# New duration and hand-over constants in the list schedule of a four-layer image kernel

## The chip, the cores and the metric

One Trainium2 chip, of which the kernel uses one core. The metric is the device time of one execution in microseconds (us); less is better. The time before is 11614.76 us, the median of three executions (11599.19 to 11631.03). One more execution was profiled: 11598.44 us, of which 11596.7 us lie between its first and its last instruction (the span).

## The reference, cut to what matters

The input `x` has 32 images of 512 channels and 32 by 32 pixels, in float32. Four layers follow each other, and each adds its result to its input: `x = x + layer(group_norm(x))`.

```python
# layer 0: 2-D DCT of every channel, normalised, averaged; a two-layer perceptron gives one factor a channel
weights = sigmoid(relu(x_avg @ w1.T) @ w2.T);  return x * weights[:, :, None, None]
# layer 1: grouped 3x3 convolution, 32 groups
# layer 2: 1x1 conv -> x, z;  f1 = 1x1 conv(x), f2 = 2x2/2 conv(f1), f3 = 2x2/2 conv(f2)
def step(h, inp):                     # state-space scan along the pixels, 256 channels x 16 states
    da, dbx, c = inp
    h = h * da + dbx
    return (h, einsum('bdn,bn->bd', h, c))
# run forward and backward on f1, f2, f3; layer norm; the coarse results are added to the finer ones;
# times silu(z), and a last 1x1 conv
# layer 3: channel attention from a deformable 3-tap sampling over the channel means
```

The scan of layer 2 is the heart of the work: for each image 256 channels by 16 states by 1024 pixels in two directions on `f1`, and the same on the smaller `f2` and `f3`.

## The kernel before

**A plan, then the program.** The kernel does not write its instructions down in the order in which the text stands. It first records operations with `pe`, `act`, `dve`, `pool` and `dma`, one helper for each engine (matrix, scalar, vector and GpSimd engine, and the queue SP that issues DMAs). Each record has a duration that the author states, a key (when it is due, in hundredths of an image), and the buffers that it reads and writes. Then `Plan.order` plays a list schedule: it keeps a clock, lets each engine take the ready operation with the lowest key, marks it as busy for the stated duration, and releases the operations that depend on it after a hand-over time. The order in which operations are taken becomes the program order of every engine's queue, and the same pass gives each buffer its slot. On the chip each queue runs strictly in that order and waits on semaphores. So the stated durations and hand-over times cost nothing themselves; they decide only who stands before whom, and which slot a buffer has.

**The constants.** `SAME` is the hand-over to the same engine, `CROSS` to another engine within the scan loops (`fine` and `both`), `BESIDE` to another engine everywhere else, `QUEUE` to an operation that issues a DMA. `t_mm`, `t_dve`, `t_act` and `t_pool` turn a number of elements into a duration; many matrix operations have a number of their own.

The lines where the plan uses them:

```python
for u in o.users:
    u.waits -= 1
    if not u.waits:
        lat = self.SAME if u.eng == o.eng and o.eng != "SP" else u.cross
        heapq.heappush(events, (now + lat, u.seq, 0, u))
...
if e == "SP":
    idle[e] = now + o.dur
    dma = max(dma, now + 2.0) + o.size / 240e3
    o.end = dma + 1.2
else:
    idle[e] = o.end = now + o.dur
```

**One scan unit.** An image has 84 units of 128 partitions by 1024 elements: 32 for the forward scan on `f1` (`fine`, first half), 20 for the coarse scans of the next image (`lower`, through `both`), 32 for the backward scan on `f1` (`fine`, second half). A unit on `f1` is this chain: the matrix engine spreads B into the PSUM buffer `pb` (L1220, two matmuls), ACT makes the decay `da` by an exponential (L1227), DVE multiplies `pb` by `dt` (L1233) and scans (L1166, `h` from `da` and `pb`), POOL multiplies `h` by C (`cb`, L1241), and after each four units the matrix engine adds four `h` into the accumulators `y0` and `y1b` (L1249). In the coarse scans the same steps have the lines L1347 and L1354, L1389 and L1398, L1361, L1409 and L1419. There are two `pb`, two `da`, two `cb`, six `h`, four `dt`, and one of each accumulator; a unit can begin only when the unit that held its slot is through.

**Work beside.** All other work is laid between the units by its key: the transforms of layer 0 three images ahead (`spectra`, L455 to L639; images after the fourth are taken in groups of four), the grouped convolution of layer 1 (`front`, L853), the dense layers (`dense`, L906; `down_conv`, L928), the inputs of the scans (`prepare`, L1013 to L1075), the layer norms (L1096 to L1119), the output (L1494 to L1511) and layer 3 (`back`, L1552 to L1658; its twelve weighted sums an image are L1618 on ACT and L1624 on DVE). The keys, such as `FRONT` or `LN_LATE`, and the choice of engine for each operation are not touched.

Of the kernel before, what the change touches and what calls it, by code (L numbers as in the profile page):

```python
# [59 lines left out]
class Plan:  # L60
# [3 lines left out]

    SAME, CROSS, BESIDE, QUEUE = 0.06, 0.2, 0.5, 2.0

    def __init__(self, rings):
        self.rings = rings  # L70
# [45 lines left out]
    def order(self):  # L116
# [35 lines left out]
        while events:  # L152
            now = events[0][0]
            touched = set()
            while events and events[0][0] <= now:
                _, _, kind, o = heapq.heappop(events)
                if kind == 0:
                    heapq.heappush(ready[o.eng], (o.key, o.seq, o))
                    touched.add(o.eng)
                elif kind == 1:  # L160
                    touched.add(o)
                else:
                    done += 1
                    for b in o.bufs:
                        b.left -= 1
                        if b.ring and not b.left:
                            free[b.ring].append(b.slot)
                            wake(b.ring, touched)
# [5 lines that stand above are left out]
            again = True  # L174
            while again:
                again = False
                for e in engines:
                    while idle[e] <= now and ready[e]:
                        _, _, o = heapq.heappop(ready[e])
                        n = lacks(o)  # L180
                        if n is not None:
                            parked[n].append(o)
                            continue
                        woken = set()
                        o.acq = [b for b in o.acq if b.slot is None]
                        for b in sorted(o.acq, key=lambda b: b.key):
                            b.slot = free[b.ring].pop(0)
                            if b.ring in line:
                                line[b.ring].pop()
                                wake(b.ring, woken)  # L190
                        again = again or bool(woken)
                        o.start = now
                        issued.append(o)
                        if e == "SP":
                            idle[e] = now + o.dur
                            dma = max(dma, now + 2.0) + o.size / 240e3
                            o.end = dma + 1.2
                        else:
                            idle[e] = o.end = now + o.dur
                        heapq.heappush(events, (idle[e], o.seq, 1, e))  # L200
                        heapq.heappush(events, (o.end, o.seq, 2, o))
        stuck = [o for o in self.ops if o.start is None]
# [14 lines left out]


def t_mm(n, count=1):
    return count * (1.0 * n / 512 + 0.03)  # L220


def t_dve(n):
    return 0.075 + n / 960


def t_act(n, ptr=False):
    return 0.09 + n / 1180 + (0.06 if ptr else 0.0) + (0.12 if n > 1000 else 0.0)


def t_pool(n):
# [4 lines left out]
def kernel(ctx: ExitStack, tc: tile.TileContext, t: dict, out: bass.AP):  # L236
# [228 lines left out]
    def root(dst, v, n, bufs, key):  # L465

        pool(
            lambda: nc.gpsimd.tensor_tensor(dst(), v(), mhalf[:, 0:n], ALU.pow), 175, bufs, bufs, key
        )

    def group_stats(mean, var, gm, rstd, q, w, key, read, write, n=CT):


        ps = mm()
        pe(
            lambda: nc.tensor.matmul(ps.t[:, 0:n], lhsT=gavg, rhs=mean(), start=True, stop=True),
            0.25, read, [ps], key,
        )
        dve(lambda: nc.vector.tensor_sub(q(), mean(), ps.t[:, 0:n]), n, [*read, ps], write, key)
        act(lambda: nc.scalar.copy(gm(), ps.t[:, 0:n]), n, [ps], write, key)  # L480
        act(lambda: nc.scalar.activation(q(), q(), AF.Square), n, write, write, key)
        p2 = mm()

        def sums():
            nc.tensor.matmul(p2.t[:, 0:n], lhsT=gavg, rhs=q(), start=True, stop=False)
            nc.tensor.matmul(p2.t[:, 0:n], lhsT=gavg, rhs=var(), start=False, stop=True)

        pe(sums, 0.5, [*read, *write], [p2], key)
        dve(lambda: nc.vector.tensor_scalar_add(w(), p2.t[:, 0:n], 1e-5), n, [p2], write, key)
        root(rstd, w, n, write, key)  # L490

# [15 lines left out]
    def spectra(b, k0, k1):  # L507
        for c in range(CT):
# [37 lines left out]
            for step in range(2):  # L546


                for h in range(2 * step):
                    ps = mm()  # L550

                    def turn(ps=ps, h=h, sx=sx):
                        for j in range(4):
                            i = (h * 4 + j) * P
                            nc.tensor.transpose(
                                ps.t[:, j * P : (j + 1) * P], sx.t[:, 0, i : i + P], ident
                            )

                    pe(turn, 0.7, [a], [ps], key)
                    act(  # L560
                        lambda ps=ps, h=h, sx=sx: nc.scalar.copy(sx.t[:, 1, halves[h]], ps.t), HB,  # L561
                        [ps], [z[h]], key,
                    )
                for h in range(2):
# [7 lines left out]
                                start=True, stop=True,  # L572
                            )

                    pe(dcts, 1.05, [z[h], *([st] if step == 0 else [])], [ps], key)
                    if step == 0:
                        def put(ps=ps, h=h, sx=sx, b=b, c=c):
                            dst = sx.t[:, 0, :].rearrange("p (k r) -> p r k", k=IMG)
# [71 lines left out]
    def channel_weights(b0, n, key):  # L650
# [8 lines left out]
        for h in range(2):  # L659
            w, wf = weights(b0)  # L660
            dma(
                lambda wf=wf, h=h: nc.sync.dma_start(
                    wf().rearrange("p (c m) -> p c m", c=CT), t["w1"][:, :, h * HB : (h + 1) * HB]
                ),
                P * 8192, [], [w], key,
            )
            ps = mm()
            for m in range(4):
                def up(wf=wf, ps=ps, m=m):
                    for c in range(CT):  # L670
                        nc.tensor.matmul(
                            ps.t[:, m * n : (m + 1) * n],
                            lhsT=wf()[:, c * HB + m * P : c * HB + (m + 1) * P],
                            rhs=sg.t[:, 0:n, 2, c], start=(c == 0), stop=(c == CT - 1),
                        )

                pe(up, 0.9, [w, *st], [ps], key)
            act(
                lambda ps=ps, h=h: nc.scalar.activation(
                    sm.t[:, h * 4 * n : (h + 1) * 4 * n], ps.t[:, 0 : 4 * n], AF.Relu  # L680
                ),
                4 * n, [ps], [(sm, "hid")], key,
            )
        for h in range(2):
# [8 lines left out]
            for m in range(2):  # L693
                for k0 in (0, 4):
# [5 lines left out]
                                start=(k == 0), stop=(k == 7),  # L700
                            )

                    pe(down, 0.9, [w, (sm, "hid")], [ps], key)
            e = slice(8 * n, 10 * n)
            sigmoid_to(
                lambda h=h: sg.t[:, 0:n, 5, 2 * h : 2 * h + 2],
# [20 lines left out]
    def front(b, S, k0, k1):  # L727
# [38 lines left out]
                        start=True, stop=True,  # L766
                    )

        pe(blocks, 1.2, [sm], [ps], k0, [sk])
        act(lambda ps=ps: nc.scalar.copy(sk.t[:, 0:48], ps.t[0:96, 0:48]), 48, [ps], [(sk, 0)], k0)  # L770

        def by_block(i):
# [21 lines left out]
        for c in range(CT):  # L794
# [44 lines left out]
            for h in range(2):  # L839
# [9 lines left out]
                for n, dy in enumerate((1, 0, 2)):  # L849
# [11 lines left out]
                                start=(n == 0), stop=(n == 2),  # L861
                            )

                    pe(conv, 1.2, [wk, pk], [ps], key, [xb])


                act(
# [33 lines left out]
    def dense(w, rhs, m, cols, reads, ps, key, acq=(), opened=False):  # L901


        for k, r in enumerate(rhs):
# [3 lines left out]
                    start=(k == 0 and not opened), stop=(k == len(rhs) - 1),  # L908
                )

            pe(f, t_mm(HB), [*reads[0], reads[1][k]], [ps], key, acq)

    def down_conv(lv, f, side, S, key):

# [4 lines left out]
        for m in range(2):  # L919
            ps = mm()  # L920
            for k in range(2):
                for q0 in (0, 2):
# [8 lines left out]
                                start=(k == 0 and q == 0), stop=(k == 1 and q == 3),  # L931
                            )

                    pe(part, 2 * max(t_mm(n), 0.25), [w, f], [ps], key, [fo])
            act(
                lambda m=m, ps=ps: nc.scalar.activation(
                    fo.t[:, m, :], ps.t[:, 0:n], AF.Identity, bias=c_b[lv - 1][:, m : m + 1]
# [248 lines left out]
    def fine(lv, f, pre, S, rev, ck):  # L1186
# [8 lines left out]
        for d in range(2):  # L1195
# [10 lines left out]
            for k in range(NS // NQ):  # L1206
# [7 lines left out]
                for q in range(4):  # L1214
# [3 lines left out]
                    def bcast(pb=pb, k=k):  # L1218
# [15 lines left out]
                        [dt[q], pb], [pb], ck.key(DB_AHEAD),  # L1234
                    )
                    pl.op(
                        "DVE", 2.2, lambda h=h, da=da, pb=pb: scan(h.t, da.t, pb.t, rev), [da, pb], [h],
                        ck.key(),
                    )
                    pool(  # L1240
# [5 lines left out]
                for i, cols in enumerate(halves):  # L1246
# [4 lines left out]
                                start=(k == 0), stop=(k == NS // NQ - 1),  # L1251
                            )

                    pe(add, 1.15, hs, [acc[i]], ck.key(2))
            y = pl.buf("yv")
            yv.append(y)
            dma(
# [45 lines left out]
    def both(lv, f, pre, ysum, below, n, ck):  # L1303
# [24 lines left out]
        for d in range(2):  # L1328
# [11 lines left out]
            for k0 in range(0, 4, nk):  # L1340
# [15 lines left out]
                                start=True, stop=True,  # L1356
                            )

                pe(bcast, 0.6 if nk == 1 else 0.8, [sb], [pb], ck.key(B_AHEAD))
                dve(  # L1360
                    lambda pb=pb, quads=quads: nc.vector.tensor_mul(  # L1361
                        pieces(pb.t),
# [16 lines left out]
                for r in range(2):  # L1379
# [14 lines left out]
                    else:  # L1394
# [7 lines left out]
                                n, [(dt, 1)], [(da, q)], ck.key(6), True,  # L1402
                            )
                    pl.op(
                        "DVE", 2.2, lambda h=h, da=da, pb=pb, r=r: scan(h.t, da.t, pb.t, r == 1),
                        [da, pb], [h], ck.key(),
                    )
                    pool(
# [13 lines left out]
                                    start=(k0 + k == 0), stop=False,  # L1422
                                )

                    pe(add, 0.65 if nk == 1 else 1.4, [h], [acc[r]], ck.key(2))
                    ck.u += 1
            dg = skip_weights(lv, d, ck.key(8))
            for r in range(2):
# [1 line left out]
                    lambda r=r, d=d, dg=dg: nc.tensor.matmul(  # L1430
                        accv(r)[:, d, 0:n], lhsT=dg.t, rhs=f.t[:, d, :], start=False, stop=True
                    ),
                    max(t_mm(n), 0.22), [f, dg], [acc[r]], ck.key(2),
                )
        y = pl.buf("yv" if n > 64 else "yc")

# [87 lines left out]
    def back(b, S, k0, k1):  # L1524
        sm, xo = S["smb"], S["xo"]

        def at(i):
            return k0 + (k1 - k0) * i
# [29 lines left out]
                ps.t[:, 2 * CT : 3 * CT], lhsT=ident, rhs=yv(), start=True, stop=True  # L1558
            )

        pe(shift, 1.1, n_, [ps], at(0.2))
        for i in range(3):
            def op_(i=i):
                return npos()[:, 4 * i : 4 * i + 4]
# [31 lines left out]
                    rhs=ident, start=True, stop=True,  # L1596
                )

        pe(rows, 1.2, n_, [ps2], at(0.2), [gt])
        act(lambda: nc.scalar.copy(gt.t[:, 0, :], ps2.t), HB, [ps2], [(gt, 0)], at(0.2))  # L1600

        for c in range(CT):
            for i in range(3):
# [3 lines left out]
                def hat():  # L1607
# [17 lines left out]
                        pr.t, in0=pr.t, in1=gt.t[:, 0, :], op0=ALU.mult, op1=ALU.add, scale=1.0,  # L1625
                        scalar=0.0, accum_out=vv()[:, 4 * i + c : 4 * i + c + 1],
                    ),
                    640, [(gt, 0), pr], [pr, (sm, "v")], key,
                )
        av, e = v(66), v(0)  # L1630
        k = at(0.85)
# [201 lines left out]
```

## Time and profile before

| | before |
|---|---|
| median of the runs | 11614.76 us |
| profiled execution | 11598.44 us, span 11596.7 us |
| mean granted clock of the matrix engine | 0.862 |
| scans (L1166) on DVE | 2688, 2276 ns each, 6070.7 us |
| products (L1233) on DVE | 2048, 1219 ns each, 2462.8 us |
| products (L1241) on POOL | 2048, 2363 ns each, 4820.2 us |
| exponentials (L1227) on ACT | 2048, 1145 ns each, 2339.5 us |
| spreading matmuls (L1220) on the matrix engine | 4096 records, 427 ns each, 1394.1 us |
| DMA | 2116.76 MB, 183 GB/s on the mean |

Busy times are those of the engine itself; waits are not in them. A group's mean duration holds the tail of the instruction's pipeline, in which the next instruction has already begun, so the distance from start to start is a little less. Matmuls in float32 leave two records each.

### The profile page before, as it was taken

The page shows a single profiled execution, that of the slowest core. Times are in us where ns is not written, and L with a number is a line of the kernel's source. Part 1 is how long each engine was busy: PE and PEld are TensorE (multiplying, and loading weights), DVE is VectorE, ACT ScalarE, POOL GpSimd, SP SyncE. Part 2 cuts the span into 40 slices and gives each one's busy share as a digit, 9 for nine tenths or more (in the row PEclk, how much of TensorE's full clock was granted, in tenths as well). Part 3 has the DMA queues.
Part 4 walks back from the last instruction along what each step waited for, and adds up shares of the span by engine and source line. Part 5 has one row for each costly group of instructions (what it writes and reads, how often), then busy time and mean ns, then how long its engine had stood idle before and what let it go on. Part 6 is the DMA issues. An engine that isn't in the chain of part 4 may idle for free. (4 is left out here: it accounts for less than half of the span.)

```text
span 11596.7 us, 151995 instructions
## 1 busy us (share of the span) xinstructions
PE 9343.7 (81%) x47512; PEld 4101.9 (35%) x47512; DVE 9951.1 (86%) x8869; ACT 8256.8 (71%) x15681; POOL 9555.2 (82%) x7755
## 2 busy tenths in 40 slices
PE   6788888888888888888888788888888888787765
PEld 4344334334333333333333333333433333222221
DVE  1775987998899988999889889889889989989997
ACT  4677777777677767777777777777677776767664
POOL 1776877888888888888889878888888889888885
PEclk7788888988899988898889888888789888888877
DMA  4666666777777767776677767667676677776654
GB/s 130 163 176 165 170 184 178 190 190 197 191 197 189 188 180 200 196 196 181 185 187 209 191 177 185 182 185 200 181 201 183 177 193 191 200 191 180 167 140 135
DMA packets 931008, 2116.76 MB, mean 183 GB/s; under 512 B 240027, under 2 KB 372531, under 8 KB 917779
## 3 DMA queue, kind: packets, MB, share of 16 engines
q1 hardware_dynamic: 920992, 2103.45, 68.3%
q8 instruction: 377, 6.18, 0.2%
q10 hardware_dynamic: 9206, 3.59, 0.1%
q14 instruction: 433, 3.55, 0.1%
HBM read 1676.98 MB, written 429.52 MB: 182 GB/s over the span
## 5 line engine op out<-in xcount | busy, mean ns | idle before, releaser
L1166 DVE TENSOR_TENSOR_SCAN h<-da,pb 128x1024 f32<-128x1024 f32 x2688 | 6070.7, 2276 | 345.5 <-PE y1b L1249 84.4
L1241 POOL TENSOR_TENSOR h<-h,cb 128x1024 f32<-128x1024 f32 x2048 | 4820.2, 2363 | 988.8 <-DVE h L1166 655.9
L1227 ACT ACTIVATE da<-dt,w_Al 128x1024 f32<-128x1024 f32 x2048 | 2339.5, 1145 | 1442.6 <-DVE h L1166 1155.0
L1233 DVE TENSOR_TENSOR pb<-dt,pb 128x1024 f32<-128x1024 f32 x2048 | 2462.8, 1219 | 333.0 <-PE pb L1220 281.2
L1220 PE MATMUL pb<-sb,sel_b 96*128 96x512 bf16 x4096 | 1394.1, 427 | 1046.3 <-DVE h L1166 958.6
L1409 POOL TENSOR_TENSOR h<-h,cb 128x1024 f32<-128x1024 f32 x640 | 1510.4, 2364 | 13.4 <-DVE h L1166 3.1
L1220 PEld LDWEIGHTS <-sel_b 96*128 96x128 bf16 x4096 | 404.7, 107 | 2203.9 <-issue 2166.0
L906 PE MATMUL mm<-x,wt 128*128 128x512 f32 x2048 | 1025.5, 623 | 69.4 <-ACT f L963 16.5
L853 PE MATMUL mm<-pk,wk 99*32 99x512 f32 (+1 forms) x6144 | 908.1, 677 | 88.6 <-DMA pk<-in_xp 31.5
L1398 ACT ACTIVATE da<-dt,w_Al 128x255 f32<-128x255 f32 x2048 | 900.2, 503 | 99.1 <-DVE h L1166 86.9
L1249 PE MATMUL y<-h,w_sel_y 128*32 128x512 f32 x4096 | 801.3, 744 | 37.0 <-POOL h L1241 29.9
L570 PE MATMUL mm<-w_dct,sx 128*128 128x128 f32 x3968 | 616.5, 309 | 99.8 <-ACT sx L561 24.0
L570 PEld LDWEIGHTS mm<-w_dct,sx 128*128 128x128 f32 x3968 | 554.0, 216 | 305.2 <-ACT sx L561 67.0
L1249 PE MATMUL y1b<-h,w_sel_y 128*32 128x512 f32 x4096 | 661.7, 678 | 0.0
L906 PE MATMUL mm<-y,w_out_w 128*128 128x512 f32 x1024 | 573.0, 649 | 2.4 <-POOL y L1299 2.2
L906 PEld LDWEIGHTS mm<-x,wt 128*128 128x128 f32 x2048 | 379.8, 196 | 499.2 <-issue 272.3
L1066 POOL TENSOR_TENSOR g<-g,g 128x512 f32<-128x512 f32 (+2 forms) x384 | 393.1, 1024 | 153.2 <-ACT g L1065 146.1
L1050 PE MATMUL mm<-xd,dtw 64*128 64x512 f32 (+2 forms) x768 | 428.1, 643 | 90.6 <-ACT xd L1020 11.2
L1096 PE MATMUL mm<-ln,ones_d 128*128 128x512 f32 (+1 forms) x768 | 425.5, 654 | 72.9 <-ACT ln L1108 26.8
L1361 DVE TENSOR_TENSOR pb<-dt,pb 128x1024 f32<-128x1024 f32 x320 | 388.6, 1217 | 79.6 <-PE pb L1347 59.7
L928 PE MATMUL mm<-f,wt 128*128 128x256 f32 (+1 forms) x1984 | 409.9, 353 | 21.2 <-DVE yv L1107 7.3
L1096 PE MATMUL mm<-yv,ones_d 128*128 128x512 f32 x640 | 391.9, 713 | 38.0 <-DVE y L1119 5.2
(288 smaller groups left out, 16109.1 us busy)
## 6 DMA issues: line engine op xcount, KB each, us to landing
dt<-dd SPq DMA_DIRECT2D x2048, 256.0 KB, 7.5
cb<-cd SPq DMA_DIRECT2D x2048, 128.0 KB, 5.0
pk<-in_xp SPq DMA_DIRECT2D x768, 297.0 KB, 5.6
dd<-g SPq DMA_DIRECT2D x256, 512.0 KB, 5.8
xr<-x SPq DMA_DIRECT2D x128, 512.0 KB, 6.8
yv<-fs SPq DMA_DIRECT2D x128, 512.0 KB, 5.2
dt<-ddm SPq DMA_DIRECT2D x512, 128.0 KB, 4.0
sx<-in_x SPq DMA_DIRECT2D x124, 512.0 KB, 5.1
```

The source lines that it names most:

```text
L570: nc.tensor.matmul(ps.t[:, j * P : (j + 1) * P], lhsT=sx.t[:, 1, i : i + P], rhs=dct, start=True, stop=True,)
L853: nc.tensor.matmul(ps.t[32 * q : 32 * q + 32, r0 * IMG : r1 * IMG].rearrange("p (r k) -> p r k", k=IMG), lhsT=wk.t[:, q, 32 * dy : 32 * dy ...
L906: nc.tensor.matmul(ps.t, lhsT=w(k)[:, m * P : (m + 1) * P], rhs=r()[:, cols], start=(k == 0 and not opened), stop=(k == len(rhs) - 1),)
L1096: lambda d=d: nc.tensor.matmul(ps.t[:, 0:n], lhsT=ones_d, rhs=of(d), start=(d == 0), stop=(d == 1)),
L1166: nc.vector.tensor_tensor_scan(v[0], v[1], v[2], 0.0, ALU.mult, ALU.add)
L1220: nc.tensor.matmul(pb.t[:, cols], lhsT=sel_b[:, k, :], rhs=sb.t[:, cols], start=True, stop=True,)
L1227: lambda da=da, z=dt[q], k=k, g=g: nc.scalar.activation(da.t, z.t[:, 1, :], AF.Exp, scale=A[lv][:, k, g : g + 1]),
L1233: lambda pb=pb, z=dt[q]: nc.vector.tensor_mul(pb.t, z.t[:, 0, :], pb.t), HW,
L1241: lambda h=h, cb=cb: nc.gpsimd.tensor_mul(h.t, h.t, cb.t), HW, [h, cb], [h],
L1249: nc.tensor.matmul(acc[i].t[q * 32 : (q + 1) * 32, :], lhsT=sel_y, rhs=hs[q].t[:, cols], start=(k == 0), stop=(k == NS // NQ - 1),)
L1398: lambda da=da, quads=quads, q=q, g=g, body=body, k0=k0: nc.scalar.activation(pieces(da.t)[:, 0, q, body], quads(1)[:, q, body], AF.Exp, s ...
L1409: lambda h=h, k0=k0: nc.gpsimd.tensor_mul(pieces(h.t), pieces(h.t), cbv()[:, k0 : k0 + nk, :].rearrange("p k (o l) -> p k o l", o=1).to_br ...
```

## The change

Only numbers that the plan reads are changed. Every engine still has the same instructions of the same shapes in the same number: 8871 on DVE, 14071 on ACT, 7760 on POOL, 31566 on the matrix engine, 8332 on SP. Their order changes on all five, from the first operations on, and with it which slot of a ring a buffer takes.

The hand-over times fall to half or less. A matrix operation now releases those who wait for it 0.14 us after the engine is free again. Durations of matrix operations mostly rise; those of DVE and of short ACT operations rise by a few hundredths; the power operation on POOL (`root`) is put at 240 elements and not 175.

```diff
-    SAME, CROSS, BESIDE, QUEUE = 0.06, 0.2, 0.5, 2.0
+    SAME, CROSS, BESIDE, QUEUE = 0.06, 0.1, 0.2, 1.0
+    DRAIN = 0.14
...
-                            idle[e] = o.end = now + o.dur
+                            idle[e] = now + o.dur
+                            o.end = idle[e] + (self.DRAIN if e == "PE" else 0.0)
...
 def t_mm(n, count=1):
-    return count * (1.0 * n / 512 + 0.03)
+    return count * (0.06 + 1.02 * n / 512)
 def t_dve(n):
-    return 0.075 + n / 960
+    return 0.11 + n / 970
 def t_act(n, ptr=False):
-    return 0.09 + n / 1180 + (0.06 if ptr else 0.0) + (0.12 if n > 1000 else 0.0)
+    return 0.125 + n / 1180 + (0.06 if ptr else 0.0) + (0.06 if n > 1000 else 0.0)
...
-            lambda: nc.gpsimd.tensor_tensor(dst(), v(), mhalf[:, 0:n], ALU.pow), 175, bufs, bufs, key
+            lambda: nc.gpsimd.tensor_tensor(dst(), v(), mhalf[:, 0:n], ALU.pow), 240, bufs, bufs, key
...
-        pe(sums, 0.5, [*read, *write], [p2], key)
+        pe(sums, 0.59, [*read, *write], [p2], key)
...
-                    pe(turn, 0.7, [a], [ps], key)
+                    pe(turn, 0.8, [a], [ps], key)
...
-                    pe(dcts, 1.05, [z[h], *([st] if step == 0 else [])], [ps], key)
+                    pe(dcts, 1.15, [z[h], *([st] if step == 0 else [])], [ps], key)
...
-                pe(up, 0.9, [w, *st], [ps], key)
+                pe(up, 1.28, [w, *st], [ps], key)
...
-                    pe(down, 0.9, [w, (sm, "hid")], [ps], key)
+                    pe(down, 1.16, [w, (sm, "hid")], [ps], key)
...
-        pe(blocks, 1.2, [sm], [ps], k0, [sk])
+        pe(blocks, 0.4, [sm], [ps], k0, [sk])
...
-                    pe(conv, 1.2, [wk, pk], [ps], key, [xb])
+                    pe(conv, 1.12, [wk, pk], [ps], key, [xb])
...
-            pe(f, t_mm(HB), [*reads[0], reads[1][k]], [ps], key, acq)
+            pe(f, 0.97, [*reads[0], reads[1][k]], [ps], key, acq)
...
-                    pe(part, 2 * max(t_mm(n), 0.25), [w, f], [ps], key, [fo])
+                    pe(part, 2 * max(0.93 * t_mm(n), 0.285), [w, f], [ps], key, [fo])
...
-                        "DVE", 2.2, lambda h=h, da=da, pb=pb: scan(h.t, da.t, pb.t, rev), [da, pb], [h],
+                        "DVE", 2.21, lambda h=h, da=da, pb=pb: scan(h.t, da.t, pb.t, rev), [da, pb], [h],
...
-                    pe(add, 1.15, hs, [acc[i]], ck.key(2))
+                    pe(add, 1.3, hs, [acc[i]], ck.key(2))
...
-                pe(bcast, 0.6 if nk == 1 else 0.8, [sb], [pb], ck.key(B_AHEAD))
+                pe(bcast, 0.55 if nk == 1 else 0.58, [sb], [pb], ck.key(B_AHEAD))
...
-                    pe(add, 0.65 if nk == 1 else 1.4, [h], [acc[r]], ck.key(2))
+                    pe(add, 0.6 if nk == 1 else 0.69, [h], [acc[r]], ck.key(2))
...
-                    max(t_mm(n), 0.22), [f, dg], [acc[r]], ck.key(2),
+                    max(t_mm(n), 0.29), [f, dg], [acc[r]], ck.key(2),
...
-        pe(shift, 1.1, n_, [ps], at(0.2))
+        pe(shift, 1.38, n_, [ps], at(0.2))
...
-        pe(rows, 1.2, n_, [ps2], at(0.2), [gt])
+        pe(rows, 1.45, n_, [ps2], at(0.2), [gt])
...
-                    640, [(gt, 0), pr], [pr, (sm, "v")], key,
+                    500, [(gt, 0), pr], [pr, (sm, "v")], key,
```

The spreading of B on `f1` (`bcast` in `fine`) keeps its 0.55 us, and `t_pool` its formula. The new lines move the source down: a line Ln of before is L(n+1) between L68 and L200 and L(n+2) after that.

More of the change, by code (lines that the diff above doesn't have):

```diff
@@ L1404, in both @@
                     pl.op(
-                        "DVE", 2.2, lambda h=h, da=da, pb=pb, r=r: scan(h.t, da.t, pb.t, r == 1),
+                        "DVE", 2.21, lambda h=h, da=da, pb=pb, r=r: scan(h.t, da.t, pb.t, r == 1),
                         [da, pb], [h], ck.key(),
```

## The prediction, made before the changed kernel was run

> **What bounds the kernel now.** I read the page first: no engine is full, but DVE leads with 86%.
>
> ```profile
> span 11596.7 us, 151995 instructions
> PE 9343.7 (81%) x47512; PEld 4101.9 (35%) x47512; DVE 9951.1 (86%) x8869; ACT 8256.8 (71%) x15681; POOL 9555.2 (82%) x7755
> DVE  1775987998899988999889889889889989989997
> ```
>
> The first DVE digit shows the start: the first scan comes at 332.5 us, with 296 us of DVE idle before it. The rest of its 1636 us of idle time lies inside the scan stream. Who ended it stands in the waits of DVE (total, times, longest):
>
> ```profile
> DVE pb L1233 <- PE pb L1220: 281.2, 238, 6.1
> DVE sms L617 <- POOL sms L611: 139.9, 18, 19.3
> DVE mm L1624 <- ACT mm L1618: 95.9, 65, 17.1
> DVE h L1166 <- PE y1b L1249: 84.4, 66, 6.0
> ```
>
> Two kinds mix here. The first row is many short waits (1.2 us each) for the matrix engine's spreading. The second is 18 waits with a longest of 19.3 us: side work of layer 0, which hurts only because DVE had nothing else in front of it. I looked these places up in the timeline of DVE:
>
> ```profile
> 6720.45 1.23 DVE L1233 TENSOR_TENSOR pb<-dt,pb 128x1024 f32<-128x1024 f32 x1 [0.51 <-PE pb L1220]
> 6725.20 1.29 DVE L1107 TENSOR_TENSOR yv<-yv,mm 128x512 f32<-128x512 f32 x2 [3.52 <-PE mm L1096]
> 6731.08 0.16 DVE L479 TENSOR_TENSOR smb<-smb,mm 128x4 f32<-128x4 f32 x1 [4.53 <-PE mm L476]
> ...
> 6758.00 2.28 DVE L1166 TENSOR_TENSOR_SCAN h<-da,pb 128x1024 f32<-128x1024 f32 x1
> ```
>
> The product at 6720 is done, and its scan comes 36 us later, behind 30 side instructions (layer norm, layers 0 and 3), each waiting for another engine. I call it a starved stretch: in the order no scan is due, so the list is filled with whatever dribbles in. After the first scan, before's DVE order has seven runs of 15 or more side instructions. The windows give these seven, each from scan to scan, and a run of 11 at 7769 that also waited (length; busy and count of PE, PEld, DVE, ACT, POOL; clock, DMA share, GB/s):
>
> ```profile
> 923.70:1051.40 127.70, 107.95 (x478) 61.34 (x478) 26.29 (x78) 90.47 (x194) 46.42 (x68) 0.80 0.44 134
> 1736.60:1829.00 92.40, 77.31 (x363) 47.37 (x361) 20.72 (x62) 57.59 (x146) 30.66 (x55) 0.85 0.38 123
> 666.40:710.50 44.10, 41.26 (x206) 30.78 (x204) 12.97 (x25) 24.52 (x65) 27.90 (x34) 0.77 0.48 149
> 5670.30:5705.40 35.10, 28.41 (x142) 11.43 (x134) 14.11 (x30) 22.71 (x47) 22.45 (x28) 0.90 0.49 135
> 6027.40:6050.10 22.70, 19.00 (x66) 8.15 (x62) 8.86 (x20) 10.08 (x23) 17.90 (x27) 0.68 0.51 151
> 6717.50:6758.00 40.50, 31.57 (x118) 16.76 (x117) 14.08 (x36) 32.04 (x65) 25.59 (x33) 0.87 0.26 92
> 7769.30:7785.80 16.50, 15.18 (x64) 6.49 (x63) 8.70 (x19) 12.61 (x27) 14.24 (x17) 0.70 0.68 179
> 9500.20:9524.80 24.60, 17.75 (x61) 8.27 (x60) 11.46 (x26) 18.22 (x33) 17.56 (x21) 0.72 0.17 52
> ```
>
> Length less DVE is the idle time: 101.4, 71.7, 31.1, 21.0, 13.9, 26.4, 7.8 and 13.1 us, 286 together. In the first three, the start-up of the pipeline of images, PE is 84 to 94% busy and is the bound; the last five lie seven units into the backward scan, and there it is 72 to 92%.
>
> **The change, part by part.** Nothing is added or removed, so busy times stay, and only idle time can move. I compare the two orders, which can be read without times.
>
> *Starved stretches.* Five gone: those at 5670 (24 side instructions), 6027 (15), 6717 (30), 7769 (11) and 9500 (17) have no counterpart; the new order holds no run of over 10 after scan 250. Gain 21.0+13.9+26.4+7.8+13.1 = 82.2 us. At 666 the run falls from 21 to 9: 31.1 x 12/21 = 17.8. At 1736 (53 before scan 304) it goes too, but PE was the bound there, and the new order puts 60 us more PE work between scans 104 and 300 (803 against 743 by the groups' busy time for each instruction), where DVE has 747: the 71.7 us come back as short waits. I take 0 and keep 71.7 as the other end. Against it: a new run of 28 before scan 246, at 0.88 us an instruction (47.4 us over 54 at 5670 and 6717) 24.6; 77 for 72 at 923, 5 x 1.41 = 7; runs of 6 to 10 rise from 14 to 28, at 1.18 us of idle each on the mean of before's, 16.5. Sum: 100 - 48 = 52 us gained, 124 with the other end.
>
> *Evenness elsewhere.* I gave each instruction its group's busy time over its count and summed for every four consecutive units what each engine's order puts between them. The excess of an engine over DVE, summed and divided by 4, falls on PE from 697 to 634 us, on POOL from 545 to 540, on ACT from 412 to 363. What such an excess costs I fitted to before's own intervals between scans: 0.29 us per us on PE, 0.91 on POOL, 0.82 on ACT. So 63 x 0.29 + 5 x 0.91 + 49 x 0.82 = 63 us gained (57 to 88 with three or five units). This sees the same stretches from another side and is not added: between 52 to 124 (mean 88) and 63 I take 75.
>
> *Spreading.* A `pb` is free when its scan ends; the matrix engine spreads the next into it (0.59 us for both matmuls where the clock is full), and then DVE may multiply. Where DVE's order puts less than 0.95 us between that scan and that product it must wait: 72 places before, 85 after; what is missing sums to 47.9 and 65.6 us. With 1.5 us needed (PE still in a dense matmul) it is 234 and 258, with 2.0 549 and 578. Loss 18 to 29, I take 24. Behind the waiting product stand all scans of DVE; POOL and the additions wait for those.
>
> *Durations.* Some come nearer to the rows, some do not. The sampled sum (L1624) goes from 0.742 to 0.625, and two of its records stand 0.62 us apart; `blocks` from 1.2 to 0.4 (24 records, 0.47 an image). But after a product's start at 5015.43 the next instruction began at 5016.56, 1.13 us later, where the plan had 1.142 and now has 1.166. No instruction runs differently, so these cost nothing beyond the order counted above.
>
> *Hand-overs.* A scan that ended at 5014.93 released a matmul at 5014.98: 0.05 us. The new 0.1 and 0.2 are nearer than 0.2 and 0.5. But what a hand-over had too much was slack for whoever is late. I set it at 0 and price it as a rival.
>
> *SP.* All 8332 instructions stay, many change places, so a load may now stand behind another's wait. Landing `dt` made DVE's products wait 45.3 us in all; I take 0 and plus or minus 45 for the range. At the start, PE has the same 559 instructions before the first spreading in both orders and DVE the same 134 before the first scan; ACT has six more before its first exponential (4 us of work), hidden by PE, which is busy for 203 of the first 300 us while ACT is for 126. I take 0, and 4 us if that cover is gone.
>
> Sum: 11598.4 - 75 + 24 = 11547 us for an execution like the profiled one. That lies 16 us under the median of the three runs, so the forecast for a median is 11564 us, 0.4% less.
>
> [...] The additions (L1249) are now put at 1.30 us. In the trace the same eight records took 1.93 us in the first of these windows and 1.05 in the second (the clock is the third number from the end):
>
> ```profile
> 4999.50:5003.50 4.00, 4.00 (x18) 0.70 (x17) 3.11 (x3) 3.57 (x8) 3.64 (x3) 0.50 0.59 180
> 5016.00:5018.10 2.10, 2.02 (x18) 0.49 (x17) 2.10 (x4) 2.10 (x5) 2.10 (x2) 1.00 0.91 249
> ```
>
> [...]
>
> **The rivals.** 0.3% (35 us) is about what a measurement of this kernel can tell from no change.
>
> *Slower: the slack was worth more than the exactness* (chance 0.30). Outside the eight windows and the start, DVE waited 242 times before side instructions (305 us). If each now comes 0.3 us nearer to its producer (0.5 to 0.2) and waits that much longer, and the starved stretches only turn into bare idle time, it costs 242 x 0.3 = 73, plus 29 for the spreading: 11614.8 + 102 = 11717 us. It decides once the gain falls under these. For it: DVE's order is not the cause of starvation, what feeds the scan is. Against it: DVE could not use that slack, the runs were filled already.
>
> *No change: the work is only moved* (0.20). What 1736 us shows holds everywhere: PE, 81% busy, sets the pace, and each stretch that goes comes back as short waits. Of the 75, 0 to 25 are left, and the 24 are lost: 11614 to 11639 us.
>
> *The numbers are not the means they claim* (within the above). By the products' 1.166 against 1.13 the plan thinks DVE slower by 0.036 x 74 = 2.7 us an image and may feed it late by as much; at most 32 x 2.7 = 86 us, inside the slower case.
>
> **How the numbers follow.** Forecast 0.50: faster, around 11564; its own range, from a gain of 124 + 45 less 18 to none but the threshold, is 11464 to 11580. With the slower case up to most of its 11717, and a little below for a start-up that gains too, 8 in 10 lie in 11440 to 11690. Chances: faster 0.50, same 0.20, slower 0.30.
>
> **What would show it.** Right: busy times as before to 1%; in DVE's timeline no run of over 10 side instructions after 2000 us; the wait of L617 for L611 well under 139.9 us; that of L1233 for L1220 at 281 plus about 24. Wrong: more idle time before L1166 (345.5 us) or L1233 (333.0) than the stretches give back, above all for `y1b` or the spreading; or a first scan later than 332.5 us.

## The result and the profile after

The changed kernel's median is 11531.22 us over four runs (11523.79 to 11538.17) against 11619.4 us of before over four: a ratio of 0.9926, interval 0.9909 to 0.9943, which is 86 us less (the two medians lie 88 apart). The forecast was 11564, 51 us under the median of three in the section on the time before. The profiled execution took 11523.79 us, 74.7 less than before's.

The page's first lines and DVE's row:

```profile
span 11521.9 us, 151927 instructions
PE 9362.7 (81%) x47512; PEld 4085.7 (35%) x47512; DVE 9954.0 (86%) x8869; ACT 8238.1 (71%) x15681; POOL 9544.7 (83%) x7755
DVE  1775889988898988989989999899899999998997
```

Busy times are those of before within 0.4%, DVE's within 3 us. All of the gain is idle time: what DVE waits before its instructions fell from 1635.9 to 1558.3 us. The same stretches, now from scan to scan at the same scan numbers, in the order of the eight shown of before, and a ninth with the new run before scan 246 (length; busy and count of PE, PEld, DVE, ACT, POOL; clock, DMA share, GB/s):

```profile
945.10:1081.20 136.10, 113.26 (x550) 63.45 (x548) 28.81 (x82) 93.11 (x213) 48.62 (x72) 0.87 0.45 136
1785.70:1790.10 4.40, 3.54 (x14) 1.56 (x13) 4.40 (x4) 1.63 (x2) 4.40 (x5) 1.00 1.02 277
691.90:715.10 23.20, 20.71 (x120) 15.91 (x120) 8.44 (x14) 10.47 (x31) 13.27 (x17) 0.72 0.42 122
5689.30:5694.30 5.00, 5.00 (x28) 1.11 (x24) 2.93 (x5) 4.97 (x10) 4.62 (x6) 0.54 0.40 118
6043.70:6048.50 4.80, 3.19 (x21) 1.84 (x22) 4.80 (x8) 3.53 (x8) 4.43 (x4) 1.00 0.72 207
6714.30:6720.70 6.40, 5.01 (x21) 1.86 (x14) 6.40 (x9) 5.65 (x9) 4.79 (x3) 0.98 0.22 82
7746.00:7755.10 9.10, 7.94 (x31) 2.30 (x30) 6.53 (x11) 9.10 (x14) 7.76 (x6) 1.00 0.30 100
9432.60:9440.20 7.60, 5.38 (x18) 1.53 (x16) 7.60 (x13) 7.08 (x11) 7.36 (x6) 0.88 0.07 20
1512.80:1549.20 36.40, 30.00 (x125) 12.20 (x121) 16.96 (x34) 30.57 (x58) 17.21 (x20) 0.72 0.43 122
```

Length less DVE: 107.3, 0, 14.8, then 2.1, 0, 0, 2.6, 0 for the five in the steady part, and 19.4 for the new one. The waits of DVE that answer to those shown:

```profile
DVE pb L1235 <- PE pb L1222: 238.7, 232, 4.7
DVE sms L619 <- POOL sms L613: 118.8, 33, 14.7
DVE h L1168 <- PE y1b L1251: 82.4, 59, 6.2
...
DVE mm L1626 <- ACT mm L1620: 59.2, 58, 4.4
```

Sorted by how many side instructions stand between two products or scans, DVE's idle time changed like this (us, from the two traces):

| side instructions between | before | after |
|---|---|---|
| more than 10 | 266.7 | 119.4 |
| 6 to 10 | 16.5 | 49.4 |
| 3 to 5 | 164.8 | 119.4 |
| 1 or 2 | 310.1 | 375.3 |
| none | 521.5 | 529.1 |
| ahead of the first scan | 295.8 | 309.8 |

The long runs gave back 147 us, and shorter waits took 60 of it again; the start took 14.

By distances between scans, the profiled executions differ like this (us, after less before): up to the first scan +15.6, scans 0 to 104 +2.1, 104 to 304 -56.5, 304 to 1254 +27.7, 1254 to the last -58.0, behind the last -5.8. So the part between scans 304 and 1254 became slower, although a starved stretch went from it too (that at 5670).

### The profile page after: what moved, and what is told of

It reads as the page before. It is cut to its first block, busy times and chain, and to the rows that moved or that the text cites. A ratio compares the mean times of both kernels' runs of the same rounds, so it can differ in the third digit from the quotient of the medians.

```text
span 11521.9 us, 151927 instructions
## 1 busy us (share of the span) xinstructions
PE 9362.7 (81%) x47512; PEld 4085.7 (35%) x47512; DVE 9954.0 (86%) x8869; ACT 8238.1 (71%) x15681; POOL 9544.7 (83%) x7755
## 5 line engine op out<-in xcount | busy, mean ns | idle before, releaser
L1235 DVE TENSOR_TENSOR pb<-dt,pb 128x1024 f32<-128x1024 f32 x2048 | 2461.7, 1218 | 313.5 <-PE pb L1222 238.7
L855 PE MATMUL mm<-pk,wk 99*32 99x512 f32 (+1 forms) x6144 | 924.2, 686 | 95.5 <-DMA pk<-in_xp 32.9
```

Source lines behind the costliest of these rows:

```text
L855: nc.tensor.matmul(ps.t[32 * q : 32 * q + 32, r0 * IMG : r1 * IMG].rearrange("p (r k) -> p r k", k=IMG), lhsT=wk.t[:, q, 32 * dy : 32 * dy ...
L1235: lambda pb=pb, z=dt[q]: nc.vector.tensor_mul(pb.t, z.t[:, 0, :], pb.t), HW,
```

## The experiments

Theories at the outset. **B**: the gain comes from `BESIDE`; 0.5 us, where a scan handed over to a matmul in 0.05 us, makes the plan deliver every link of a side chain late, and chains that feed the scans then starve them. **D**: it comes from durations nearer to the rows. **L**: another order of the same work lands elsewhere by luck. Each kernel below was timed beside before on the same chip. Evenness prices are those of the prediction; the figures given with e2 to e7 were worked out for five consecutive units, though e2 and e6 say four.

### e1 and e4: one number, both ways

```diff
-    SAME, CROSS, BESIDE, QUEUE = 0.06, 0.2, 0.5, 2.0
+    SAME, CROSS, BESIDE, QUEUE = 0.06, 0.2, 0.2, 2.0   # e1;  e4: 1.0 in the third place
```

> Before with one number changed: BESIDE 0.2 in place of 0.5; all durations and the other hand-overs as before. Theory B (the gain comes from BESIDE, which makes the plan delay every link of the side chains that feed the scans by 0.3 us too much, until DVE's list runs out of scans): the whole gain, a ratio to before of 0.990 to 0.995, and DVE idle in runs of over 10 side instructions falls from 267 us to about 100 to 130 (its order holds three such runs, of 17, 67 and 12, 96 instructions in place of 276). Theory D (the gain comes from durations that are nearer to the rows): 0.998 to 1.002. Theory L (luck: any other order of this kernel lands somewhere within half a per cent): no value is excluded, but e1 to e4 should then show no relation to BESIDE.

> Before with one number changed the other way: BESIDE 1.0 in place of 0.5. Theory B: slower by about as many us for each 0.1 as e1 gains, or more: 1.010 to 1.025, with DVE idle in runs of over 10 side instructions at 400 us or more (its order holds 20 such runs with 498 side instructions; the evenness price says +255 us). Theory D: 0.998 to 1.002 or any small change. Theory L: within 0.993 to 1.007.

e1: 0.9955 (0.9943 to 0.9968). e4: 1.0365 (1.0349 to 1.038), twice what B had asked for. DVE's idle time in runs of over 10 went from 266.7 us to 115.3 in e1 and 659.5 in e4. B's direction holds both ways; both sizes lie outside its ranges. D, which gave 1.00 for both, does not hold. In e1 60% of the after kernel's gain is there (52 of 86 us), and not the whole: the long runs gave back 151 us, and shorter waits after the first scan took 117 of it again. e4's stretch before scan 304, where before had 92.4 us and after 4.4:

```profile
1720.00:1979.50 259.50, 193.48 (x984) 105.43 (x984) 38.77 (x114) 137.07 (x325) 67.68 (x125) 0.78 0.50 145
```

The first scan of image 4's coarse part comes 253 us after its predecessor (the window starts 7 us ahead of that). No engine is full: PE is busy 75% of it, ACT 53%. DVE's side instructions wait there for other engines in turn, most of all L617 for POOL's L611 (66.7 us in five waits). That these waits are the links of one long chain is an inference; it was not followed link by link.

### e2 and e3: after with the old BESIDE, and the durations alone

```diff
 # e2, after with
-    SAME, CROSS, BESIDE, QUEUE = 0.06, 0.1, 0.2, 1.0
+    SAME, CROSS, BESIDE, QUEUE = 0.06, 0.1, 0.5, 1.0
 # e3, after with
+    SAME, CROSS, BESIDE, QUEUE = 0.06, 0.2, 0.5, 2.0
+    DRAIN = 0.0
```

> After with BESIDE back at 0.5; every other new number stays. Theory B: the gain is gone, a ratio to before of 0.999 to 1.008; its order holds eight long runs with 273 side instructions, as many as before's 276, and the evenness price used in the prediction would make it 106 us slower than before at four units. Theory D: the gain stays, 0.990 to 0.995. Theory L: anywhere between 0.993 and 1.007.

> Before with the new durations alone; the four hand-over times as before and no 0.14 us after a matrix operation. Theory B: no gain, 0.997 to 1.004 (seven long runs with 215 side instructions, evenness price +15 us). Theory D: 0.990 to 0.995. Theory L: anywhere between 0.993 and 1.007.

e2: 1.0039 (1.0026 to 1.0053). e3: 0.999 (0.9981 to 0.9999). So with all other new numbers in place, `BESIDE` at 0.2 and not 0.5 is worth 0.9926 / 1.0039 = 0.9887. e2's stretch before scan 304:

```profile
1736.10:1919.00 182.90, 148.27 (x668) 84.29 (x663) 32.27 (x96) 117.08 (x268) 58.97 (x98) 0.81 0.47 138
```

Side by side, the distances between scans (us, from the traces):

| kernel, BESIDE | scans 104 to 303 | 303 to 304 | 1254 to the last |
|---|---|---|---|
| before, 0.5 | 939.5 | 92.3 | 5800.8 |
| e3, 0.5 | 943.0 | 133.6 | 5723.8 |
| e2, 0.5 | 938.2 | 182.9 | 5794.3 |
| e4, 1.0 | 944.9 | 252.6 | 5970.3 |
| after, 0.2 | 970.9 | 4.4 | 5742.8 |
| e1, 0.2 | 984.8 | 34.0 | 5770.8 |

The stall before scan 304 goes with `BESIDE` in all six. The other kernels agree: it is 4.5 to 33.9 us in those with 0.05 to 0.22, and 60.3 to 166.9 us in those with 0.49 to 0.52. With 0.2 the 200 scans ahead of it take 31 to 45 us longer, so part of it comes back as short waits, and part is gone for good. The durations alone save 77 us after scan 1254, lose 41 at this stall and 24 between scans 304 and 1254: what D expected is seen in the late part only.

### e5, e6 and e7: what of the rest helps

```diff
 # e5, after with
+    SAME, CROSS, BESIDE, QUEUE = 0.06, 0.2, 0.2, 2.0
+    DRAIN = 0.0
 # e6, after with
+    DRAIN = 0.0
 # e7, before with
+    SAME, CROSS, BESIDE, QUEUE = 0.06, 0.1, 0.5, 2.0
```

> The new durations and BESIDE 0.2; CROSS 0.2 and QUEUE 2.0 as before and no 0.14 us after a matrix operation. So far BESIDE alone gave 0.9955 and the durations alone 0.999 with 58 us lost up to scan 340 and 75 gained after it. Theory B2 (BESIDE clears the start and the starved stretches, the durations help in the steady part, and the shorter CROSS takes some of it back): better than after, 0.987 to 0.991, scans 0 to 340 as in after (about 1945 us) and the rest 9440 us or less against after's 9492. Theory B (BESIDE is all, the rest is noise): 0.994 to 0.997. Theory C (CROSS 0.1 and the 0.14 us are what after has over BESIDE alone): 0.995 to 1.000.

> After with the 0.14 us that follow a matrix operation set to 0. Its order is more even than after's (the price of the prediction says 110 us less than before at four units, after 59), but 80 us are missing between a scan and the next product in the same pb where 0.95 us are needed (after 66, before 48). If the evenness price decides: 0.986 to 0.990. If those 0.14 us are real and protect DVE from waiting for the spreading: slower than after, 0.993 to 0.998, with more than after's 239 us of waits of L1235 for L1222.

> Before with one number changed: CROSS 0.1 in place of 0.2 (the hand-over within the scan loops). Theory B2: slower, 1.002 to 1.007 (evenness price +55 us, and the missing time ahead of products 79 us for 48), with more waits of products for the spreading than before's 281 us. Theory C: faster, 0.995 to 0.999. Theory L (luck): anywhere in 0.995 to 1.005.

e5: 0.9875 (0.986 to 0.9889), inside B2's range and outside those of B and C; scan 340 started 1938.6 us into the profiled execution, and from there to the last scan it took 9446.8. e6: 0.9856 (0.9839 to 0.9873), a median of 11440.99 us, the fastest of all kernels run, below before and after. e7: 1.0069 (1.0052 to 1.0087), where products waited 320.1 us for the spreading and not 281.2: both as B2 had said. The after kernel is slower with the 0.14 us after a matrix operation than without (0.9926 against 0.9856), so they bring nothing here. They hardly protect products, which waited 246 us in e6 and 239 in after:

```profile
DVE pb L1235 <- PE pb L1222: 246.1, 227, 5.5
DVE sms L619 <- POOL sms L613: 98.6, 30, 15.9
```

CROSS 0.1 loses 0.7% from before, yet sits in the fastest kernel: the numbers do not add up one by one, and B2's charge against CROSS is not borne out. e5 and e1 differ only in the durations, 0.9875 against 0.9955; e3 and before do too, 0.999. Whether the durations are worth more once `BESIDE` is at 0.2 is not shown, since the next section finds differences of this size between orders that hardly differ in their numbers. The same holds for the 0.14 us. But e3 and e5 also differ in `BESIDE` alone, and give 0.9875 / 0.999 = 0.9885 for it, beside the 0.9887 of e2 and after.

### e8, e10 and e11: how much is luck

```diff
 # e8, before with
+    SAME, CROSS, BESIDE, QUEUE = 0.06, 0.19, 0.49, 1.9
 # e11, before with
+    SAME, CROSS, BESIDE, QUEUE = 0.06, 0.21, 0.52, 2.1
 # e10, after with
+    SAME, CROSS, BESIDE, QUEUE = 0.06, 0.11, 0.22, 1.1
```

> A measure of luck: before with its three cross-engine hand-overs 2 to 5% less (0.19, 0.49, 1.9 for 0.2, 0.5, 2.0), far less than the change made, which still gives another order on every engine. If other orders by themselves move the time by as much as the change did, it lies anywhere in 0.993 to 1.007; if the size of the numbers decides, within 0.998 to 1.002.

> Luck beside before, the other way: CROSS 0.21, BESIDE 0.52, QUEUE 2.1. Evenness price +57 us (e8 had +18 and gave 1.0036). Theory E: 1.003 to 1.008. If before is a chance draw out of orders of equal worth and the price says nothing: 0.997 to 1.003.

> Luck beside after: CROSS 0.11, BESIDE 0.22, QUEUE 1.1, the rest as after; another order on every engine for a tenth of a change. Evenness price -67 us to before where after has -63. Theory E: 0.990 to 0.995, beside after's 0.9926. If after's gain is mostly a lucky order: 0.996 to 1.003.

e8: 1.0036 (1.0023 to 1.0049). e11: 1.0105 (1.0089 to 1.012). e10: 0.9895 (0.9881 to 0.9908). A change of 2 to 5% in the hand-overs moves this kernel by 0.4 to 1.1%, as much as the change under study; e11 lies outside both ranges that were given for it. Luck is real, then: before was the luckiest of the three orders around it, after the less lucky of its two. But it does not make the gain: the five kernels with `BESIDE` 0.2 or 0.22 lie between 0.9856 and 0.9955, the seven with 0.49 or more (before among them) between 0.999 and 1.0365, with no overlap. DVE's idle time in runs of over 10 side instructions divides them in the same way: 96 to 159 us in the five, 246 to 660 in the seven.

### e9 and e12: as short as the hand-over itself

```diff
 # e9, after with
+    SAME, CROSS, BESIDE, QUEUE = 0.06, 0.1, 0.05, 0.5
+    DRAIN = 0
 # e12, the same with QUEUE 1.0
```

> The new durations with hand-overs as short as the trace shows them or shorter: CROSS 0.1, BESIDE 0.05, QUEUE 0.5, nothing after a matrix operation. Chosen among eighteen orders by the evenness price at four units, worked out from the order before any run of it: -145 us to before, the lowest of all (after -63, e6 -109, e5 -126). Theory E (evenness of the order decides, luck included): faster than e6, 0.984 to 0.988. If slack is worth something once BESIDE is under the real hand-over, or QUEUE under a DMA's: slower than e6, 0.988 to 0.995.

> What made e9 (0.9978) lose against e6 (0.9856): e6 with BESIDE 0.05 in place of 0.2, and QUEUE left at 1.0. If a BESIDE under the real hand-over is too short, so that side instructions stand at the head of a queue before they can run: as e9, 0.994 to 1.000, with 380 or more waits of over 150 ns before side instructions on DVE (e9 410, e6 330). If the culprit was QUEUE 0.5, which puts stores of SP ahead of loads and lets them wait at its head: as e6, 0.983 to 0.988, with the waits of L1077 for POOL and of L1042 for ACT back from e9's 513 and 325 us to about e6's 440 and 231. Evenness price -123 us.

e9: 0.9978 (0.9966 to 0.999), a miss: by the evenness of its order it had to be the fastest. e12: 0.996 (0.9947 to 0.9973), so QUEUE was not the cause, or not alone; of the two waits named for SP, that of L1042 for ACT came back (217.6 us) and that of L1077 for POOL did not (563.6). Against e6 both have more waits of over 150 ns before side instructions on DVE (410 and 417, e6 330), as e12 had named for a `BESIDE` that is too short.

Put together, the pairs of kernels that differ in `BESIDE` alone show both sides of the number. "Side waits" are DVE's waits of over 150 ns before side instructions outside the long runs; all columns but the ratio are in us, from the traces.

| pair | `BESIDE` | ratio | DVE's idle time in runs of over 10 | side waits | DVE's idle time in all |
|---|---|---|---|---|---|
| before, e4 | 0.5 to 1.0 | 1.0365 | 266.7 to 659.5 | 314.8 to 257.4 | 1635.9 to 2092.2 |
| before, e1 | 0.5 to 0.2 | 0.9955 | 266.7 to 115.3 | 314.8 to 418.0 | 1635.9 to 1593.8 |
| e2, after | 0.5 to 0.2 | 0.9887 | 343.5 to 119.4 | 299.2 to 356.3 | 1701.3 to 1558.3 |
| e3, e5 | 0.5 to 0.2 | 0.9885 | 265.7 to 134.5 | 295.3 to 360.8 | 1626.8 to 1513.9 |
| e6, e12 | 0.2 to 0.05 | 1.0106 | 96.3 to 67.6 | 344.4 to 420.5 | 1469.1 to 1593.8 |

In all five pairs the shorter `BESIDE` comes with longer side waits and shorter long runs. From 0.5 to 0.2 the long runs give more than the side waits take; from 0.2 to 0.05 they have little left to give. That is where the slower rival lives: side instructions that stand late at the head of DVE's queue, 417 waits of over 150 ns in e12 and 330 in e6. That they hold up the scans behind them fits the rest of the 125 us between e6 and e12 (waits before scans and products are 81 us longer), but was not followed from wait to wait, and a difference of 1% is no larger than e11's from before.

## Why the prediction was right or wrong, point by point

The sign and the range were right, and 51 us were forecast where 86 came. Part of that is luck: the term for 1736 was 57 us too low, that for the spreading had the wrong sign (24 lost, 31 gained), the start lost 16 that stood at 0, and neighbouring orders lie 36 us from after (e10) and 42 and 122 us from before (e8, e11). By its steps:

- **Five starved stretches in the steady part**: 82.2 us forecast, 77.5 measured (82.2 less the 4.7 that the windows show). But from scan 304 to the last, DVE's idle time fell by 41 us only (930.6 to 889.6), so 36 of the 77.5 came back there as shorter waits.
- **The stretch at 666**: 17.8 forecast, 16.3 measured. **At 923**: 7 lost, 5.9 measured. **The new run before scan 246**: 24.6 lost, 19.4 measured. Pricing a run by its instructions, from the rows of its own kind, was good to some 5 us each.
- **The stretch at 1736** is the term that was mis-sized. I took 0 of its 71.7 us of idle time, since PE was 84% busy there and would hand it back as short waits. The distance between scans 303 and 304 fell by 88 us, and the 200 scans ahead grew by 31: 57 net. The mechanism was there, but the work was counted to scan 300 and so left out the stretch itself. From scan 104 to 304, before first:

```profile
797.10:1829.00 1031.90, 852.04 (x4320) 411.01 (x4320) 774.16 (x788) 731.35 (x1444) 747.24 (x641) 0.85 0.64 173
814.80:1790.10 975.30, 810.18 (x4232) 389.32 (x4230) 765.70 (x754) 700.78 (x1387) 726.00 (x617) 0.88 0.67 180
```

PE is 83% busy in both, but for 42 us less. About half of that is 88 records fewer (21 us at before's mean durations; they stand elsewhere in its order), the rest the same kinds of records taking less time, with the granted clock at 0.88 and not 0.85. Only 15 of the 57 us are idle time of PE. e1 fits the forecast better: 1018.8 against 1031.8 us from scan 104 to 304, 13 gained.
- **Runs of 6 to 10**: 16.5 lost, 32.9 measured.
- **Spreading**: 24 lost by the count of tight places. The waits of products for it fell by 42.5 us (281.2 to 238.7), those of the coarse products rose by 11.3 (59.7 to 71.0). The count of places was no measure; what decides instead was not looked into. The 0.95 us of that count lies between two measured times: in before's trace, where the spreading followed its scan at once, a product that waited for it began 0.68 us after that scan's end at a granted clock of 1.0 (median of 19) and 1.10 us at 0.5 (13).
- **SP**: the products' waits for `dt` went from 45.3 to 67.3 us, inside the 45 allowed.
- **The start** was wrong at 0: the first scan came at 348.1 us and not 332.5. In e6, whose only other number is the 0.14 us, it came at 331.3; but e2, which has the 0.14 us, had it at 330.2, so that number alone does not make it late. Between 100 and 150 us the matrix engine's granted clock was 0.50 in after and 0.60 in before, with PE busy for 44 and 41 of 50 us. Whether the clock is cause or result here stays open.
- **Evenness**: 63 us forecast for after. The price, worked out from each order alone, against the measurement, in us to before:

| | after | e1 | e2 | e3 | e4 | e5 | e6 | e7 | e8 | e9 | e10 | e11 | e12 |
|---|---|---|---|---|---|---|---|---|---|---|---|---|---|
| price, four units | -63 | -77 | 93 | 2 | 242 | -126 | -109 | 56 | 18 | -145 | -67 | 57 | -123 |
| measured, (ratio - 1) x 11615 | -86 | -52 | 45 | -12 | 424 | -145 | -167 | 80 | 42 | -26 | -122 | 122 | -46 |

The correlation is 0.90 over all, 0.96 without e9 and e12, 0.79 without e4. The price sees how the order loads the engines, luck included; it does not see a queue's head that waits, and it failed for e9 and e12, where the side waits of over 150 ns are many (410 and 417, in e6 330).

- **The additions and the clock**: before's trace has 812 stretches of granted clock, 406 at 0.5 and 406 at 1.0. In the prediction's two windows an addition's eight records took 1.93 us at 0.50 and 1.05 at 1.00, and the plan's 1.30 us lies between them. What moves the clock from one to the other no run shows. e5 against e1 gives the new durations 0.9875 / 0.9955 = 0.992, e3 against before 0.999. Neighbouring orders differ as much, and the durations were not tried engine by engine, so whether those of the matrix engine bring something stays open.
- **The rivals**: the slack that was set at 0 had a price. DVE's side waits of over 150 ns, the long runs included, fell from 574.6 to 471.8 us, but outside the long runs they rose from 314.8 to 356.3, and in e1, with `BESIDE` alone, to 418.0: 103 us, where the slower rival had said 73. It lost because the starved stretches did not turn into bare idle time. "Only moved" held for 60 of 147 us, in e1 for 117 of 151.
- **The signs**: as forecast, busy times stayed within 1%, and no run of over 10 came after 2000 us. The wait of L617 for L611 went from 139.9 to 118.8 us, but 79.8 and 77.4 of it lie ahead of the first scan; behind that it fell from 60.1 to 41.4. The products' wait for the spreading fell where it was to rise. One sign of being wrong came up, the first scan later than 332.5 us.

## What to carry to other kernels

In a list schedule the stated hand-over is a knob of its own. In this kernel a scan handed over to the spreading in 0.05 us (median of 766 in before's trace). With `BESIDE` at 0.5 and 1.0 us DVE idled for 266.7 and 659.5 us in long runs of side work (before, e4); with 0.05 in place of 0.2 its side waits outside them went from 344.4 to 420.5 us (e6, e12). The best of the values tried (0.05, 0.2, 0.5 and 1.0) was 0.2 us, about four times that hand-over. Before timing, count in each engine's order the runs of side work that interrupt the main stream, and price how unevenly the engines are loaded over a few units. And time a few neighbours a few per cent away before a single setting is praised: a tenth of the change moved this kernel by as much as the change.

## What was not expected of the hardware

That so little in the plan moves so much on the chip: with the same instructions, and with busy times on DVE, ACT and POOL within 0.1%, 2 to 5% in three planned hand-over times made 0.4 and 1.1% of the median time (e8, e11). The executions of one order lie within 0.1 to 0.5% of each other (after: 11523.79 to 11538.17 us; before, beside e11: 11583.46 to 11639.31). The matrix engine's busy time did not stay the same across the kernels: 9297 us at a mean granted clock of 0.867 in e6, 9344 at 0.862 in before, 9420 and 9432 in e8 and e11, 9593 at 0.839 in e4. Whether the clock is a part of the cause there or follows from the waits stays open; before and after have the same 0.862.
